# Second attention of a two-layer gated block: the last batch's head layout made on TensorE instead of by DRAM, and its last batches routed in groups of 2, 1 and 1

## The chip, the cores and the metric

The kernel runs on one core of one Trainium2 chip. The metric is the device time of one execution in microseconds (us). The program was run three times; the profile is of one further execution. The engines are TensorE (PE, matmuls into the PSUM memory; its weight loads are shown as PEld), VectorE (DVE), ScalarE (ACT), GpSimd (POOL) and SyncE (SP, which here only issues transfers).

## What is computed

The input x has 16 batches of 128 tokens and 256 features. Two gated layers are applied:

- layer 0: cross-attention with quantized weights and a feed-forward block, each added with a tanh gate;
- layer 1: a second attention and a mixture of eight experts.

The second attention is what matters here. It has 32 heads of 8 features in 8 groups; four heads of a group share keys and values. In the reference, shortened:

```python
q = (Q @ w_q.T).reshape(B, S, G, HG, HD)
k = (K @ w_k.T).reshape(B, S, G, HD)
v = (V @ w_v.T).reshape(B, S, G, HD)
scores = jnp.einsum('bnghd,bmgd->bnghm', q, k) / scale
attn = jax.nn.softmax(jnp.where(causal, scores, NEG_INF), axis=-1)
out = jnp.einsum('bnghm,bmgd->bnghd', attn, v).reshape(B, S, D)
x = x + tanh(g) * (out @ w_o.T + b_o)
```

Then each of the 2048 tokens goes to one expert, by the largest logit. An expert takes at most 256 tokens, in the order of the tokens; so the place of a token in its expert is a running count over all earlier ones. Each expert multiplies its tokens by w1 (256 to 1024), takes gelu, multiplies by w2, and the result is scaled by the gate and added.

## The kernel before, in words

The program goes through the cross-attention (to about 940 us of the span), the feed-forward block (to about 1083), the second attention (to about 1374) and the experts (to the end). The change touches the second attention and its routing.

**Items.** The second attention is a software pipeline over items n = 0 to 63 (the loop at L1192, which runs n from -2 to 70). Item n is batch b = n // 4, half c = n // 2 % 2 of the groups, and pair p = n % 2. An item is two groups of four heads on 128 tokens. In step n of the loop stand `scores(n)` (L1051: mask and scores into PSUM), `top(n)` (L1071: the maximum of each row, on DVE), `probs(n - 1)` (L1087: eight transposes on PE, two copies to eT), `exp(n)` (L1078: eight activations on ACT), `values(n - 2)`, `divide(n - 5)`, and for every fourth step `keys`, `output` and one more stage of each `route` under way.

**Values.** For each odd item, `values` (L1102) multiplies the probabilities of a half, that is four groups q, in one PSUM tile `ps_pv` with one buffer. The weights of a group, `vg` (L1046), are 32 columns wide: value features in the even columns, ones in the odd ones, zero behind. So rows 32q to 32q+15 of the tile hold values and sums in turn, with the four heads side by side along the free axis (512 columns). The output projection needs another layout: one row for each head and feature. So the tile is copied by ACT (`og`, L1115), written by four transfers of SP to DRAM (`ods`, L1119), and read back by one (`ov`, L1127) as 128 rows of 128 values and 128 sums.

**Division and output.** `divide` (L1130) takes the reciprocal of the sums on DVE (L1138) and multiplies on POOL (L1139) into `oT`. `output(b)` (L1141) multiplies both halves of oT with the output weights on PE (L1145), adds the bias (`t`, L1147) and the gated residual (L1151) into the batch's row of a token tile `row`. That tile is made by the first batch of a routing group, from a tag with two buffers. Batch b's output stands in step 4b + 9.

**Routing.** `ROUTES` (L851) lists groups of batches as (first, count). `route` (L855) is a generator of stages, started when the last batch of its group has its output; the loop advances each by one stage a step, and what is left is drained behind the loop (L1223). Its stages: layer norm of the rows (L142 to L148, with two small activations L185 and L186); transposes (L159, L160); logits (L868); softmax, choice of the expert and running count `cum` (L879 to L894); positions by two small matmuls (L897, L898); slots (L903 to L913), then for each batch an indirect scatter of the rows to `disp` in DRAM by POOL (L915) and a plain copy of the row to the output by SP (L926). The running count orders the groups. Before the scatter a copy of token numbers is put into the tile (L910), which also must wait until the tile's buffer is free. In the second attention's PSUM pool the tag "mm" has one buffer, used in the order of the program by query projections, `output`, the logits and the positions.

**Experts.** Each expert's load `xe` (L1244) waits for all scatters, since every token may be among them. The weights of the first two experts are loaded long before.

**Order.** [...] The framework that builds the program orders the instructions by its own estimate of when they are ready, so an engine's queue is not simply the order of the text; the trace shows, for example, the slots of one routing group in turn with the layer norm of the next.

Of the kernel before, what the change touches and what calls it, by code (L numbers as in the profile page):

```python
# [9 lines left out]
F32 = mybir.dt.float32  # L10
# [5 lines left out]
ALU = mybir.AluOpType  # L16
AX = mybir.AxisListType

P = 128
B = 16  # L20
# [15 lines left out]
def flamingo_kernel(  # L36
# [27 lines left out]
    nc = tc.nc  # L64
# [4 lines left out]
    NH, NG, HD = 32, 8, 8  # L69
# [22 lines left out]
    def ps_acc(shape):  # L92
        return ps("acc", shape, 1)
# [160 lines left out]
    with (  # L254
# [80 lines left out]
        class Unit:  # L335
# [164 lines left out]
            def scores(self, c):  # L500
                qT = self.qT.pop(c)
                pscore = ps_sc([P, 4, P])
                for j in range(4):
                    nc.tensor.matmul(  # L504
                        pscore[:, j, :], qT[:, j, :], self.kT[:, 2 * c + j // 2, :],
                        start=True, stop=True,
                    )
                self.sc[c] = pscore

            def top(self, c):  # L510
                mx = small.tile([P, 4], F32, tag="mx", name="mx")
                nc.vector.tensor_reduce(mx, self.sc[c], AX.X, ALU.max, negate=True)  # L512
                self.mx = mx
# [16 lines left out]
            def divide(self, c):  # L530
                e, sums = self.e[c]
                nc.gpsimd.tensor_tensor(  # L532
                    e, e, sums[:, :, None].to_broadcast([P, 4, P]), ALU.mult
                )

            def probs(self, c):
                e, _ = self.e.pop(c)
                pt = ps_tr([P, 4, P])
                for j in range(4):
                    nc.tensor.transpose(pt[:, j, :], e[:, j, :], ident)  # L540
                eT = ap.tile([P, 4, P], F32, tag="eT", name="eT")
                nc.scalar.copy(eT, pt)  # L542
                self.eT[c] = eT

            def values(self, c):
                eT = self.eT.pop(c)
                pv = ps_pv([P, 4, P])
                for g in range(2):
                    gg = 2 * c + g
                    nc.tensor.matmul(  # L550
                        pv[:, 2 * g : 2 * g + 2, :], self.vt[:, gg * P : (gg + 1) * P],
                        eT[:, 2 * g : 2 * g + 2, :], start=True, stop=True,
                    )
                self.pv[c] = pv
# [28 lines left out]
            def output(self, c):  # L583
                if c == 0:
                    self.acc = ps_acc([P, 2 * DM])
                    self.xb = ap.tile([P, DM], F32, tag="xb", name="xb")
                    src = x1[self.b] if self.cross else x_in[self.b]
                    nc.sync.dma_start(out=self.xb, in_=src)
                for j in range(4):
                    h = 4 * c + j  # L590
                    nc.tensor.matmul(  # L591
                        self.acc, self.cat[c // 2][:, h % 8, :], wpr[self.cross, c][:, j, :, :],
                        start=(h == 0), stop=(h == 15),
                    )
# [196 lines left out]
    def down(b, hd, po):  # L791
# [18 lines left out]
    rp = ctx.enter_context(  # L810
        tc.tile_pool(name="r1", bufs=2, side="right", reuse_waits="tile")
    )
    SCALE1 = 1.0 / math.sqrt(HD)
    NQ = NH // NG


    RW = 2 * DM + 2
# [30 lines left out]
    nc.vector.memset(cum, 0.0)  # L848
    slot_s = cp.tile([P, B], I32, name="slot_s")

    ROUTES = ((0, 4), (4, 4), (8, 4), (12, 3), (15, 1))  # L851
    toks = {}
    scatters, plain = [], []

# [74 lines left out]
    cq = f1.enter_context(tc.tile_pool(name="a1c", bufs=1, side="right", reuse_waits="tile"))  # L929
# [32 lines left out]
    vgs = [cq.tile([P, NG, 32], F32, name=f"vg{i}") for i in range(2)]  # L962
    for t in vgs:
        nc.gpsimd.memset(t, 0.0)
        nc.gpsimd.memset(t[:, :, 1 : 2 * HD : 2], 1.0)

    front = {}

    def load(g):
# [63 lines left out]
    kbs, vps, es, eTs, oTs, scs, mxs, ovs = {}, {}, {}, {}, {}, {}, {}, {}  # L1033

    def keys(b):

        g, j = divmod(b, G)
        f = front[g]
        tok = slice(j * P, (j + 1) * P)
        kb = ap.tile([P, KD, NQ, P], F32, tag="kb", name="kb")  # L1040
        for c in range(KD):
            nc.gpsimd.tensor_tensor(
                kb[:, c], f["k"][:, c, None, tok].to_broadcast([P, NQ, P]),
                hmask[:, :, None].to_broadcast([P, NQ, P]), ALU.mult,
            )
        nc.gpsimd.tensor_copy(  # L1046
            vgs[b % 2][:, :, 0 : 2 * HD : 2], f["v"][:, j, :].rearrange("p (g d) -> p g d", d=HD)
        )
        kbs[b], vps[b] = kb, vgs[b % 2]

    def scores(n):  # L1051
# [50 lines left out]
    def values(n):  # L1102

        if n % 2 == 0:
            return
        b, c = n // 4, n // 2 % 2
        o = psum.tile([P, NQ * P], F32, tag="pv", name="ps_pv", bufs=1)
        for q in range(4):
            nc.tensor.matmul(
                o[32 * q : 32 * q + 32, :], vps[b][:, 4 * c + q, :],  # L1110
                eTs[n - 1 + q // 2][:, q % 2].rearrange("p h t -> p (h t)"),
                start=True, stop=True,
            )
        og = ap.tile([P, NQ, P], F32, tag="og", name="og")
        nc.scalar.copy(og.rearrange("p h t -> p (h t)"), o)  # L1115

        od = ods[n // 2]
        for q in range(4):
            nc.sync.dma_start(  # L1119
                out=bass.AP(  # L1120
                    od.tensor, od.offset + 32 * q * 2 * P,
                    [[P, 2 * HD], [2 * HD * P, NQ], [1, P]],
                ),
                in_=og[32 * q : 32 * q + 2 * HD],
            )
        ov = ap.tile([P, 2, P], F32, tag="ov", name="ov")
        nc.sync.dma_start(out=ov.rearrange("p i t -> p (i t)"), in_=od)  # L1127
        ovs[n] = ov

    def divide(n):  # L1130
        if n % 2 == 0:
            return
        b, c = n // 4, n // 2 % 2
        if c == 0:
            oTs[b] = ap.tile([P, KD, P], F32, tag="oT", name="oT")
        ov = ovs.pop(n)
        r = ap.tile([P, P], F32, tag="rsum", name="rsum")
        nc.vector.reciprocal(r, ov[:, 1, :])  # L1138
        nc.gpsimd.tensor_tensor(oTs[b][:, c, :], ov[:, 0, :], r, ALU.mult)  # L1139

    def output(b):  # L1141
        oT = oTs.pop(b)
        pw = psum.tile([P, DM], F32, tag="mm", name="ps_mm")
        for k in range(KD):
            nc.tensor.matmul(pw, oT[:, k, :], ao[:, k, :], start=(k == 0), stop=(k == KD - 1))  # L1145
        t = ap.tile([P, DM], F32, tag="t", name="t")
        nc.vector.tensor_tensor(t, pw, bo, ALU.add)  # L1147
        b0, count = next(r for r in ROUTES if r[0] <= b < r[0] + r[1])
        if b == b0:
            toks[b] = rp.tile([P, count, RW], F32, tag="row", name="row")  # L1150
        nc.vector.scalar_tensor_tensor(  # L1151
            toks[b0][:, b - b0, DM : 2 * DM], t, tg[:, 1:2], x[b], ALU.mult, ALU.add
        )
# [15 lines left out]
    for g in range(B // G):  # L1169
# [3 lines left out]
        for b in range(g * G, (g + 1) * G):  # L1173
# [8 lines left out]
    ap = f2.enter_context(tc.tile_pool(name="a1", bufs=2, side="right", reuse_waits="tile"))  # L1182
    psum = f2.enter_context(
        tc.tile_pool(
            name="psum1", bufs=1, space=bass.MemoryType.PSUM, reuse_waits="tile"
# [3 lines left out]

    N1 = 4 * B  # L1190
    routes = []
    for n in range(-2, N1 + 7):  # L1192
        if 0 <= n < N1:
            scores(n)
            top(n)
        if 0 <= n - 1 < N1:
            probs(n - 1)
        if 0 <= n < N1:
            exp(n)
        if 0 <= n < G:  # L1200
            down(B - G + n, hd, psum.tile([P, DM], F32, tag="mm", name="ps_mm"))
            if n == G - 1:
                tp.close()
                ep = ctx.enter_context(tc.tile_pool(name="e1", bufs=2, reuse_waits="tile"))
        if 0 <= n - 2 < N1:
            values(n - 2)
        if 0 <= n - 5 < N1:
            divide(n - 5)
        m = n + 2
        if m % 4 == 0 and 0 <= m < N1:  # L1210
            keys(m // 4)
        g, i = divmod(n + 12, 16)
        if 1 <= g < B // G:
            front_step(g, i)
        for stages in routes:
            next(stages, None)
        m = n - 6
        if m % 4 == 3 and 0 <= m < N1:
            output(m // 4)
            for b0, count in ROUTES:  # L1220
                if m // 4 == b0 + count - 1:
                    routes.append(route(b0, count))
    for stages in routes:  # L1223
        for _ in stages:
# [6 lines left out]
            name="psum2", bufs=2, space=bass.MemoryType.PSUM, reuse_waits="tile"  # L1231
# [6 lines left out]
    for e in range(NE):  # L1238
# [12 lines left out]
        for f in range(NFC):  # L1251
            ph = ps_mm([P, CAP])
            for k in range(KD):
                nc.tensor.matmul(
                    ph, w1t[:, k, f * P : (f + 1) * P], xT[:, k, :],
                    start=(k == 0), stop=(k == KD - 1),
# [3 lines left out]
        for c in range(NCC):  # L1260
            po = ps_sc([P, DM])
            for f in range(NFC):
                nc.tensor.matmul(
                    po, hT[:, f, c * P : (c + 1) * P], w2t[:, f, :],
                    start=(f == 0), stop=(f == NFC - 1),
# [8 lines left out]
                    ap=xe[:, c, 2 * DM + 1 : 2 * DM + 2].bitcast(I32), axis=0  # L1274
# [79 lines left out]
```

## Time and profile before

| what | value |
|---|---|
| median of 3 runs (lowest to highest) | 1501.8 us (1501.51 to 1504.62) |
| the profiled execution | 1503.01 us |
| its span, first to last instruction | 1501.3 us |
| mean granted TensorE clock | 0.966 |
| PE busy / weight loads | 1369.6 us (91%) / 964.4 us |
| DVE / ACT / POOL busy | 988.6 / 838.4 / 687.6 us |
| og to ods, 128 writes, and ods to ov, 32 reads | 32 KB and 128 KB each |

A profile line gives a start and a duration in us from the span's start, the engine, the line of the code, the operation, written tile <- read tiles, shapes, and how many instructions are merged (x8). In brackets at its end stands how long the engine had been idle before it, and what ended that. PEld is the load of weights for the matmuls of the same line, and SPq or POOLq is an engine's own queue of transfers and waits. One fp32 matmul stands as two records, a transpose as one. "128*32 128x512" is a matmul of 128 rows by 32 columns of weights that streams 512 columns.

### The profile page before, as it was taken

The page shows a single profiled execution, that of the slowest core. Times are in us where ns is not written, and L with a number is a line of the kernel's source. Part 1 is how long each engine was busy: PE and PEld are TensorE (multiplying, and loading weights), DVE is VectorE, ACT ScalarE, POOL GpSimd, SP SyncE. Part 2 cuts the span into 40 slices and gives each one's busy share as a digit, 9 for nine tenths or more (in the row PEclk, how much of TensorE's full clock was granted, in tenths as well). Part 3 has the DMA queues.
Part 4 walks back from the last instruction along what each step waited for, and adds up shares of the span by engine and source line. Part 5 has one row for each costly group of instructions (what it writes and reads, how often), then busy time and mean ns, then how long its engine had stood idle before and what let it go on. Part 6 is the DMA issues. An engine that isn't in the chain of part 4 may idle for free. (4 is left out here: it accounts for less than half of the span.)

```text
span 1501.3 us, 21652 instructions
## 1 busy us (share of the span) xinstructions
PE 1369.6 (91%) x6852; PEld 964.4 (64%) x6852; DVE 988.6 (66%) x2597; ACT 838.4 (56%) x2496; POOL 687.6 (46%) x615
## 2 busy tenths in 40 slices
PE   2789899899988999999999997999999999985998
PEld 1578778687776777777777766555544444444887
DVE  7867878778689777777676764453478787762100
ACT  3666566666656676666666663164476575741221
POOL 4476677677766565656556563121032322111111
PEclk9699999999999999999999998899999999986999
DMA  4300101000013100000000000700042212122652
GB/s 133 110 17 23 38 22 38 21 22 27 22 55 104 45 29 19 15 16 17 12 18 15 15 4 27 211 8 14 31 128 53 75 50 63 40 75 76 196 189 70
DMA packets 78770, 80.37 MB, mean 54 GB/s; under 512 B 15291, under 2 KB 64891, under 8 KB 78656
## 3 DMA queue, kind: packets, MB, share of 16 engines
q1 hardware_dynamic: 65152, 55.29, 12.7%
q10 hardware_dynamic: 11456, 17.63, 3.6%
q0 software_dynamic: 2048, 6.07, 1.1%
q8 instruction: 55, 0.90, 0.3%
q14 instruction: 59, 0.48, 0.1%
HBM read 57.14 MB, written 22.05 MB: 53 GB/s over the span
## 5 line engine op out<-in xcount | busy, mean ns | idle before, releaser
L532 POOL TENSOR_TENSOR e<-e,sums 128x512 f32<-128x512 f32 x128 | 141.4, 1105 | 239.7 <-DVE sums L528 100.8
L475 POOL TENSOR_TENSOR raw<-raw,q_r 128x512 f32<-128x512 f32 x192 | 211.3, 1126 | 21.0 <-DVE q_r L312 19.6
L520 ACT ACTIVATE e<-ps_sc,mx 128x128 f32<-128x128 f32 x512 | 181.1, 368 | 63.6 <-DVE mx L512 58.1
L452 DVE BATCH_NORM_STATS2 q_st<-raw 128x6 f32<-128x128 f32 x768 | 174.2, 279 | 64.2 <-ACT raw L443 63.6
L591 PE MATMUL ps_acc<-wp,cat 128*128 128x512 f32 x512 | 159.3, 433 | 14.0 <-POOL cat L237 13.4
L504 PE MATMUL ps_sc<-kT,qT 128*128 128x128 f32 x1024 | 140.9, 281 | 23.9 <-ACT qT L495 23.9
L542 ACT COPY eT<-ps_tr 128x512 f32<-128x512 f32 x128 | 75.3, 588 | 156.3 <-PE ps_tr L540 156.3
L504 PEld LDWEIGHTS ps_sc<-kT,qT 128*128 128x128 f32 x1024 | 132.4, 194 | 44.1 <-ACT qT L495 36.6
L237 POOL TENSOR_TENSOR cat<-e_t,e_e 128x1024 fp32r<-128x1024 bf16 x64 | 136.6, 2135 | 43.5 <-DVE e_t L231 43.5
L1082 ACT ACTIVATE e<-ps_sc,mx 128x128 f32<-128x128 f32 x512 | 139.0, 392 | 30.5 <-DVE mx L1073 30.1
L550 PE MATMUL ps_pv<-eT,vt 128*128 128x256 f32 x512 | 133.8, 383 | 1.0 <-DVE cat_y L561 1.0
L443 ACT COPY raw<-ps_mm 128x512 f32<-128x512 f32 x192 | 113.8, 593 | 29.2 <-PE ps_mm L431 25.8
L591 PEld LDWEIGHTS ps_acc<-wp,cat 128*128 128x128 f32 x512 | 94.6, 191 | 53.4 <-POOL cat L237 20.1
L486 PE MATMUL ps_tr<-ident,raw 128*128 128x128 f32 x768 | 115.2, 276 | 13.6 <-POOL raw L475 11.6
L486 PEld LDWEIGHTS ps_tr<-ident,raw 128*128 128x128 f32 x768 | 91.6, 141 | 47.5 <-POOL raw L475 20.5
L561 DVE TENSOR_TENSOR cat_y<-ps_pv,r_sm 128x512 bf16<-128x512 f32 x128 | 87.1, 680 | 47.2 <-PE ps_pv L550 46.7
L550 PEld LDWEIGHTS ps_pv<-eT,vt 128*128 128x128 f32 x512 | 97.3, 192 | 30.9 <-issue 10.5
L512 DVE TENSOR_REDUCE mx<-ps_sc 128x4 f32<-128x512 f32 x128 | 87.2, 682 | 38.5 <-PE ps_sc L504 37.8
L495 ACT ACTIVATE qT<-ps_tr,hv 128x512 f32<-128x512 f32 x128 | 101.2, 791 | 19.9 <-PE ps_tr L486 17.7
L520 ACT ACTIVATION_READ_ACCUMULATOR e<-ps_sc,mx 128x1 f32 x512 | 105.4, 206 | 0.0
L1093 PEld LDWEIGHTS ps_tr<-ident,e 128*128 128x128 f32 x512 | 59.9, 142 | 64.9 <-ACT e L1082 28.1
L1073 DVE TENSOR_REDUCE mx<-ps_sc 128x8 f32<-128x1024 f32 x64 | 77.6, 1212 | 30.2 <-PE ps_sc L1066 20.9
(221 smaller groups left out, 2687.0 us busy)
## 6 DMA issues: line engine op xcount, KB each, us to landing
w1t<-in_w ACTq DMA_DIRECT2D x8, 1024.0 KB
w2t<-in_w ACTq DMA_DIRECT2D x8, 1024.0 KB
disp<-empty SPq DMA_DIRECT2D x16, 257.0 KB
xe<-disp SPq DMA_DIRECT2D x8, 514.0 KB
ctx<-in_ctxT SPq DMA_DIRECT2D x32, 128.0 KB
stage<-in_wprojT SPq DMA_DIRECT2D x16, 256.0 KB
ods<-og SPq DMA_DIRECT2D x128, 32.0 KB
ov<-ods SPq DMA_DIRECT2D x32, 128.0 KB
```

What stands on the lines that cost most here:

```text
L237: ins = nc.gpsimd.tensor_tensor(dst, t[:, part], e[:, part], ALU.subtract)
L443: nc.scalar.copy(raw.rearrange("p h d -> p (h d)"), pm)
L452: nc.vector.bn_stats(self.st[:, 4 * blk + j, :], self.raws[blk][:, j, :])
L475: ins = nc.gpsimd.tensor_tensor(src, src, self.r[:, 4 * blk : 4 * blk + 4, None].to_broadcast([P, 4, P]), ALU.mult,)
L486: nc.tensor.transpose(pt[:, j, :], src[:, j, :], ident)
L495: nc.scalar.activation(dst, pt, AF.Identity, scale=hv[:, col : col + 1], bias=hv[:, col + 1 : col + 2])
L504: nc.tensor.matmul(pscore[:, j, :], qT[:, j, :], self.kT[:, 2 * c + j // 2, :], start=True, stop=True,)
L520: nc.scalar.activation(e[:, j, :], pscore[:, j, :], AF.Exp, bias=self.mx[:, j : j + 1], accum_out=sums[:, j : j + 1],)
L532: nc.gpsimd.tensor_tensor(e, e, sums[:, :, None].to_broadcast([P, 4, P]), ALU.mult)
L550: nc.tensor.matmul(pv[:, 2 * g : 2 * g + 2, :], self.vt[:, gg * P : (gg + 1) * P], eT[:, 2 * g : 2 * g + 2, :], start=True, stop=True,)
L591: nc.tensor.matmul(self.acc, self.cat[c // 2][:, h % 8, :], wpr[self.cross, c][:, j, :, :], start=(h == 0), stop=(h == 15),)
L1082: nc.scalar.activation(e[:, i, :], s[:, i // NQ, i % NQ, :], AF.Exp, bias=mx[:, i : i + 1])
```

## The change

Three things are changed.

- For the last batch, `values` makes the final layout at once. The values of a group stand in four copies of 32 columns, copy h with the features in columns 8h to 8h + 7 and zeros elsewhere (`vpad`); `ones8` is the same with ones. For each half, the four heads are accumulated in PSUM: 16 matmuls of 128 columns give the values, 16 more the sums. `divide` is called at once and reads both from PSUM, with both of its steps on DVE; the copy, the five transfers and the POOL product of a half are not there for this batch.
- Routing groups (12, 3) and (15, 1) become (12, 2), (14, 1) and (15, 1); groups of one batch use a tag `row1` with two buffers of its own.
- The loop ends at n = 65. Outputs of batches 14 and 15 both stand in its last step, before what is left of the routings is drained. Batch 14's output was already in step 65, batch 15's was in step 69.

```diff
-    ROUTES = ((0, 4), (4, 4), (8, 4), (12, 3), (15, 1))
+    ROUTES = ((0, 4), (4, 4), (8, 4), (12, 2), (14, 1), (15, 1))
...
+    ones8 = cq.tile([P, NQ, 32], F32, name="ones8")
+    vpad = cq.tile([P, NG, NQ, 32], F32, name="vpad")
+    nc.gpsimd.memset(ones8, 0.0)
+    for i in range(NQ):
+        nc.gpsimd.memset(ones8[:, i, HD * i : HD * i + HD], 1.0)
+    nc.gpsimd.memset(vpad, 0.0)
...
-        nc.gpsimd.tensor_copy(
-            vgs[b % 2][:, :, 0 : 2 * HD : 2], f["v"][:, j, :].rearrange("p (g d) -> p g d", d=HD)
-        )
+        v = f["v"][:, j, :].rearrange("p (g d) -> p g d", d=HD)
+        if b < B - 1:
+            nc.gpsimd.tensor_copy(vgs[b % 2][:, :, 0 : 2 * HD : 2], v)
+        else:
+            vp = vpad[:]
+            nc.gpsimd.tensor_copy(
+                bass.AP(vp.tensor, vp.offset, [vp.ap[0], [P, NG], [32 + HD, NQ], [1, HD]]),
+                v[:, :, None, :].to_broadcast([P, NG, NQ, HD]),
+            )
...
         o = psum.tile([P, NQ * P], F32, tag="pv", name="ps_pv", bufs=1)
+        if b == B - 1:
+            for t in range(2):
+                for h in range(NQ):
+                    for q in range(4):
+                        lhs = (vpad[:, 4 * c + q, h, :], ones8[:, h, :])[t]
+                        nc.tensor.matmul(
+                            o[32 * q : 32 * q + 32, t * P : (t + 1) * P], lhs,
+                            eTs[n - 1 + q // 2][:, q % 2, h, :],
+                            start=(h == 0), stop=(h == NQ - 1),
+                        )
+            divide(n, o)
+            return
...
-    def divide(n):
-        if n % 2 == 0:
+    def divide(n, o=None):
+        if n % 2 == 0 or (n // 4 == B - 1 and o is None):
             return
...
+        r = ap.tile([P, P], F32, tag="rsum", name="rsum")
+        if o is not None:
+            nc.vector.reciprocal(r, o[:, P : 2 * P])
+            nc.vector.tensor_tensor(oTs[b][:, c, :], o[:, :P], r, ALU.mult)
+            return
         ov = ovs.pop(n)
...
-            toks[b] = rp.tile([P, count, RW], F32, tag="row", name="row")
+            tag = "row" if count > 1 else "row1"
+            toks[b] = rp.tile([P, count, RW], F32, tag=tag, name=tag)
...
-    for n in range(-2, N1 + 7):
+    for n in range(-2, N1 + 2):
...
-        if m % 4 == 3 and 0 <= m < N1:
-            output(m // 4)
+        if n == N1 + 1:
+            ready = [B - 2, B - 1]
+        else:
+            ready = [m // 4] if m % 4 == 3 and 0 <= m // 4 < B - 2 else []
+        for b in ready:
+            output(b)
             for b0, count in ROUTES:
-                if m // 4 == b0 + count - 1:
+                if b == b0 + count - 1:
                     routes.append(route(b0, count))
```

More of the change, by code (lines that the diff above doesn't have):

```diff
@@ L1135, in divide @@
             oTs[b] = ap.tile([P, KD, P], F32, tag="oT", name="oT")
+        r = ap.tile([P, P], F32, tag="rsum", name="rsum")
[3 more added lines that the diff above has]
+            return
         ov = ovs.pop(n)
-        r = ap.tile([P, P], F32, tag="rsum", name="rsum")
         nc.vector.reciprocal(r, ov[:, 1, :])
```

## The prediction

> **What bounds the kernel now.** I read the page first: its chain that ended last covers only the final 15 us (issue, an output scatter), so it says nothing of the middle. Part 2 shows TensorE (PE) at 9 of 10 nearly everywhere, with a dent (5, then 9) near slice 36, where the granted clock falls too. Busy time by engine in 10 us stretches puts the dent where the change works:
>
> ```profile
> 1320.00:1330.00 10.00, 10.00 (x54) 4.16 (x54) 8.24 (x18) 7.94 (x27) 4.39 (x5) 1.00 0.32 105
> 1330.00:1340.00 10.00, 8.28 (x41) 3.88 (x38) 5.54 (x9) 5.40 (x18) 0.45 (x1) 0.83 0.22 67
> 1340.00:1350.00 10.00, 5.91 (x29) 3.59 (x26) 5.51 (x15) 2.06 (x5) 0.45 (x1) 0.80 0.25 67
> 1350.00:1360.00 10.00, 4.83 (x15) 3.17 (x14) 5.85 (x27) 0.22 (x1) 0.91 (x2) 0.50 0.04 15
> 1360.00:1370.00 10.00, 2.71 (x10) 2.15 (x10) 4.44 (x29) 0.88 (x4) 3.88 (x4) 0.50 0.27 105
> 1370.00:1380.00 10.00, 5.44 (x16) 4.18 (x17) 0.08 (x1) 2.79 (x5) 0.00 (x0) 0.50 0.32 105
> ```
>
> The columns are the stretch, its length, PE, weight loads, VectorE (DVE), ScalarE (ACT) and GpSimd (POOL) busy, the clock, the DMA share and GB/s. Until 1330 PE is full; from 1332 to 1374 nothing is. This is the drain of the second attention: latency bounds it, and the experts behind it can't start. A microsecond of this chain is a microsecond of the span. The timeline of the drain, cut to the links:
>
> ```profile
> 1331.81 0.15 DVE L910 COPY row<-number 128x1 int32<-128x1 int32 x1 [1.83 <-DMA disp<-row,slot_s]
> ...
> 1334.30 4.23 ACT L1082 ACTIVATE e<-ps_sc,mx 128x128 f32<-128x128 f32 x16 [2.17 <-DVE mx L1073]
> 1334.72 1.99 PEld L1093 LDWEIGHTS ps_tr<-ident,e 128*128 128x128 f32 x8 [2.55 <-ACT e L1082]
> ...
> 1336.93 0.20 PEld L1109 LDWEIGHTS ps_pv<-eT,vg 128*32 128x32 f32 x8 [0.22 <-issue]
> 1336.93 1.94 PE L1109 MATMUL ps_pv<-eT,vg 128*32 128x512 f32 x8
> ...
> 1340.50 1.79 PE L1109 MATMUL ps_pv<-eT,vg 128*32 128x512 f32 x8
> ...
> 1342.33 0.58 ACT L1115 COPY og<-ps_pv 128x512 f32<-128x512 f32 x1 [1.14 <-DMA ods<-og]
> ...
> 1347.05 0.34 SPq L1127 DMA_DIRECT2D ov<-ods  x1
> ...
> 1348.60 2.73 PE L868 MATMUL ps_mm<-wgt,rT 128*128 128x8 f32 x12 [0.35 <-ACT rT L160]
> 1351.37 0.18 DVE L879 TENSOR_REDUCE gmx<-ps_mm 128x3 f32<-128x24 f32 x1 [2.53 <-PE ps_mm L868]
> ...
> 1354.82 0.95 DVE L1138 RECIPROCAL rsum<-ov 128x128 f32<-128x128 f32 x1
> 1355.85 0.45 POOL L1139 TENSOR_TENSOR oT<-ov,rsum 128x128 f32<-128x128 f32 x1 [1.57 <-DVE rsum L1138]
> ...
> 1357.61 0.42 DVE L1147 TENSOR_TENSOR t<-ps_mm,bo 128x256 f32<-128x256 f32 x1 [1.85 <-PE ps_mm L1145]
> ```
>
> ```profile
> 1367.78 0.96 POOL L915 DMA_INDIRECT disp<-row,slot_s  x1 [3.34 <-DVE slot_s L913]
> 1370.78 28.55 SPq L1244 DMA_DIRECT2D xe<-disp  x3
> 1374.53 0.71 PEld L159 LDWEIGHTS ps_tr<-ident,xe 128*128 128x128 f32 x4 [8.36 <-DMA xe<-disp]
> ```
>
> Read downwards: the last values end at 1340.50 + 1.79 = 1342.29; their way by DRAM is issued back at 1347.05; the reciprocal starts only at 1354.82; oT of batch 15 is ready at 1356.30; its row has t at 1358.03, is scattered at 1367.78, and the experts begin at 1374.53. So the DRAM way is less than half of the 14.0 us from values to oT: the read of batch 15's first half, issued at 1344.72, releases POOL's wait at 1346.82, 2.1 us later, so the second landed near 1349.2. The rest is DVE's order: the reciprocal stands behind the softmax of group 12 to 14, which itself waits 2.53 us for PE at half clock.
>
> **The change, part by part.** The sum is made in the profiled execution, 1503.01 us with a span of 1501.3 and 1.7 around it; the median of the three runs is 1501.8, and I carry the difference over to it.
>
> *A. A buffer wait goes, and routing of 12 and 13 comes forward.* The first row above is the token tile of batch 15 taking the buffer of batches 8 to 11 and waiting for their scatters. All of DVE's queue stood behind it: max of item 62, then exp (ACT idle 2.17) and PE (2.55). The new tag has its own buffers: up to -1.8. But group (12, 2) now starts after batch 13 (t at 1329.04) and its norm falls into the same stretch: aggregation 0.17, sum 0.17, four small ones of 0.16, two rows of 0.41, 1.8 us of DVE, and two ACT ones of 0.20. Its transposes, logits (8 records of 0.112 at full clock, from L868's sixteen in 1.85) and some 13 small DVE operations of 0.18 fall into DVE gaps (2.44 us idle before 1340.17). If the norm is ahead of an item's max, all of the gain goes, and a us more; if the gaps take it, none. I take -1.0, ends -2.2 and +1.0.
>
> *B. More and smaller matmuls.* Four matmuls of 128x512 (eight records, two each) become 32 of 128x128, 64 records, twice: the zero-padded columns give each head its rows and double what is streamed. Per column group two records of 512 columns become sixteen of 128: 1024 columns to 2048. The same L1109 form takes 1.07 us for eight at full clock (1294.16) and 1.94 at half. With 0.17 for filling, double is 1.97 or 3.7: +0.9 or +1.8 for each half. The first half stands on PE between the transposes of items 62 and 63, the second starts when both copies of item 63's probabilities are there (1341.19) and no longer partly before. I take +1.3 and +0.9, together +2.2. The low end is +0.9: without A's gap PE may keep its clock, and 1.97 costs nothing against 1.94.
>
> Here a rule speaks against the change. The Trainium skill, "TensorE: Matmul & The Clock Gate", Part 3, The mechanism, says that a weight load overlaps a running matmul only when its row group differs; ours all use 128 rows. By that rule each record waits for its load: 16 x (0.107 + 0.27, the trace's load and 128-column matmul) = 6.1 us a half at full clock, 12.2 - 3.7 = +8.5 for both instead of +2.2. The row says otherwise: eight loads are over in 0.20 us while matmuls with 1.06 each run. I take the row; the same page's Part 2 allows a background buffer. The rule's value is the high end.
>
> *C. The way by DRAM goes.* Away: the og copy, four writes and a read on SP's queue for each half, and the POOL product. New on DVE: a reciprocal from PSUM, 0.95 as now from SBUF, and a product of 128x128 from PSUM: L1147's 128x256 is 0.42 and tiny ones 0.16, so 0.29. With handoffs 1.3 us from values to oT. The new wait: psum1's "mm" tag has one buffer, and output(14) stands right ahead of output(15) in it; its second oT half came at 1342.25, no earlier than the last values. I put it behind them: 0.9 us of PE, then t of batch 14 behind both division steps on DVE, 0.42. Output(15) starts 1.8 us after the values instead of 14.0: -12.2. If output(14) slips ahead: -12.7. If the division again stands 5.6 us behind a softmax (1354.82 - 1349.2): -6.6. The first half's division also frees the one "pv" buffer for the second half: 1.3 us after 1338.87 is 1340.2, before 1341.19, so hidden by the copies; if B's first half runs at half clock it shows with about 1 us. The vpad copy replaces POOL's 0.29 us copy with about 0.55 (between it and the 512-element product, 1.06), in idle of 5.5 us before it; it no longer waits for PE. The six new memsets, about 1.5 us (514 columns took 0.53), lie near 940 on a POOL used 1 to 3 tenths there: nothing; uncovered 1.5.
>
> *D. Two routings at the end instead of one.* Scatter of 15 follows t15 by 9.75 us now. Then positions of 12, logits and positions of 14, and logits of 15 go one after another through the single "mm" buffer: 1.3 (pl12, 1358.03 to 1359.36) + 3.6 (lg to position read, 1362.90 to 1366.47) + 4.9 (1362.90 to 1367.78) = 9.8. Norm and transposes of 15 (4.9 after t15) lie beside the first two. But DVE has some 7 us of small operations in those 4.9; about 1.9 of it delays 15: +1.9. Low end 0 (all interleave, as 12 to 14 and 15 do now); high end +7, when 14 goes through before 15's norm begins. SP's extra row copy and POOL's scatters (1.27 apart) keep their number and have slack: nothing, one scatter more in line 1.3.
>
> Sum: -1.0 + 2.2 - 12.2 + 1.9 = -9.1; 1503.0 becomes 1493.9, and the median 1501.8 becomes **1492.7**. From the scatter on, all shifts: landing, xe load, a cold first expert, which has its weights.
>
> **The rivals.** *The routings and divisions queue up* (D at +7, or C at -6.6): -4.0, 1497.8. For: DVE is in order, and softmax stood ahead of the reciprocal. Against: the orders of the two routings interleave now. *Weight loads are not hidden* (the rule): -2.8, 1499.0, no change that shows. *Slower: the small matmuls do not run side by side in the column groups.* Then 64 records follow each other at L868's spacing, 0.214 at half clock: 13.7 us a half, 27.4 - 3.7 = +23.7 for B against -11.3 for the rest: +12.4, 1514. It decides from (3.7 + 11.3)/128 = 0.117 us a record, just above L868's 0.112 at full clock. Against: L1109's eight run together today. *It does not do what it says*, DRAM way hidden anyway: excluded but for the landing part, since the reciprocal starts late for DVE's order as well; that is the first rival.
>
> **How the numbers follow.** Forecast case 0.62 (1489 to 1495.5: A and D at their ends); queueing 0.20; loads not hidden, or another loss that cancels, 0.11; serial matmuls or a new wait elsewhere from shifted buffers and reordered queues, 0.07. About 0.2%, 3.0 us, is what a measurement can tell from none, so 1498.8 is the border of faster: 0.87; within 0.07; slower 0.06 (some of the unhidden loads at half clock). The range takes forecast and queueing, 1488.8 to 1498.8.
>
> **What would show it.** A: no DVE wait on disp near 1330, exp of 62 and 63 some 1.8 us earlier, less what group 12's norm takes. B: each batch-15 group of 64 records lasts 2 us (full) or 3.7, not 6 or more. C: output(15) within 2 us of the last values, and output(14)'s t between. D: the last scatter 11 to 12 us after t15. The drain's end, 1374.5 now, near 1365. Wrong if DVE or PE at 1330 to 1350 waits for the division, if PE before 1330 is no longer full, or if the records don't overlap.

## The result, and the profile after

The changed kernel takes 1494.03 us (median of five runs, 1491.8 to 1494.53) against 1501.8 before (median, now of five runs too); the ratio is 0.9933, 95% interval 0.9919 to 0.9948. Forecast were 1492.7 us and "faster". The interval stands for 7.8 to 12.2 us saved, so it is faster; 9.1 us were forecast. The two medians alone differ by 7.8 us, which is the low edge of that interval. The profiled execution took 1494.03 us with a span of 1492.3, so 9.0 us less span than before.

Busy time by engine in stretches of 10 us, with the columns as before:

```profile
1330.00:1340.00 10.00, 9.25 (x104) 5.62 (x103) 9.37 (x20) 5.85 (x22) 0.91 (x2) 1.00 0.28 85
1340.00:1350.00 10.00, 6.78 (x90) 5.16 (x89) 8.64 (x47) 1.88 (x7) 1.48 (x3) 0.85 0.08 26
1350.00:1360.00 10.00, 4.14 (x17) 3.54 (x17) 4.75 (x39) 0.58 (x3) 2.88 (x3) 0.50 0.20 79
1360.00:1370.00 10.00, 4.11 (x11) 3.18 (x12) 0.00 (x0) 2.41 (x4) 0.00 (x0) 0.50 0.40 134
```

The clock holds at 1.00 through 1330 to 1340, where it was 0.83, and DVE is busy 9.37 of 10 us there (5.54 before): the drain's first part is now filled with work of DVE and of PE (9.25) where a stall was. The drain is one stretch shorter, with the experts starting inside the last of these.

The links of the drain from the timeline:

```profile
1330.01 0.42 DVE L1178 TENSOR_TENSOR t<-ps_mm,bo 128x256 f32<-128x256 f32 x1 [1.37 <-PE ps_mm L1176]
...
1335.67 2.16 ACT L1097 ACTIVATE e<-ps_sc,mx 128x128 f32<-128x128 f32 x8
1335.74 0.81 PEld L1128 LDWEIGHTS ps_pv<-eT,vpad 128*32 128x32 f32 x32
1335.74 1.08 PE L1128 MATMUL ps_pv<-eT,vpad 128*32 128x128 f32 x32
...
1338.09 0.67 PE L159 MATMUL ps_tr<-ident,row 128*128 128x128 f32 x4 [0.39 <-DVE row L148]
...
1339.12 1.09 PE L1108 MATMUL ps_tr<-ident,e 128*128 128x128 f32 x8 [0.35 <-ACT rT L160]
...
1341.83 1.06 PE L1128 MATMUL ps_pv<-eT,ones 128*32 128x128 f32 x32
...
1343.05 0.96 DVE L1165 RECIPROCAL rsum<-ps_pv 128x128 f32<-128x128 f32 x1
1343.98 0.42 DVE L1178 TENSOR_TENSOR t<-ps_mm,bo 128x256 f32<-128x256 f32 x1
1344.33 0.28 DVE L1166 TENSOR_TENSOR oT<-ps_pv,rsum 128x128 f32<-128x128 f32 x1
...
1345.63 0.42 DVE L1178 TENSOR_TENSOR t<-ps_mm,bo 128x256 f32<-128x256 f32 x1 [0.17 <-PE ps_mm L1176]
...
1349.60 1.03 PE L868 MATMUL ps_mm<-wgt,rT 128*128 128x8 f32 x4
1353.75 1.00 PE L868 MATMUL ps_mm<-wgt,rT 128*128 128x8 f32 x4 [0.35 <-DVE prev L893]
...
1356.15 0.57 PE L897 MATMUL ps_mm<-oh,before 128*128 128x8 f32 x2 [1.40 <-DVE slot L907]
...
1358.66 0.96 POOL L915 DMA_INDIRECT disp<-row,slot_s  x1 [1.76 <-DVE slot_s L913]
1362.11 0.89 SPq L1280 DMA_DIRECT2D xe<-disp  x2
1365.85 0.72 PEld L159 LDWEIGHTS ps_tr<-ident,xe 128*128 128x128 f32 x4 [8.80 <-DMA xe<-disp]
```

Read downwards: t of batch 13 at 1330.01; the last values end at 1341.83 + 1.06 = 1342.89; t of batch 15 ends at 1346.05, 3.2 us later where it was 15.75; the last scatter starts at 1358.66; the experts begin at 1365.85 (forecast: near 1365). No wait on `disp` is left near 1330.

One caution decides how runs are compared. Over the profiled executions of this study batch 13's t starts anywhere from 1325.0 to 1331.0, and in the changed kernel it starts 0.97 us later than before; 0.60 of that is there at 92 us already, long before anything of the edit runs. So I compare *drains*: from the start of batch 13's t to the first transposes of the experts. What follows it lasts 125.8 to 127.1 us in every run. The change's 9.0 us are then +0.97 before the drain, -9.65 in it (45.49 to 35.84) and -0.3 after it. The six new memsets and the `vpad` copy, which the prediction put at nothing, show no cost in it: batch 13's t starts at 1328.2 us on average in the nine profiles that have them, and at 1328.7 in the three without.

A second caution holds for the ends of drains. The clock falls to 0.50 at 17.0 us after the start of batch 13's t in the changed kernel's first profile and at 17.3 in e5, but at 19.8 in the changed kernel's second profile and in e9. Ends are therefore best compared with the profile whose clock falls at the same place.

All runs, in us. "V" is the end of the last values, counted like t15 (end of batch 15's t) from the start of batch 13's t:

| run | V | V to t15 | t15 to last scatter | drain | ratio to before (95%) |
|---|---|---|---|---|---|
| before | 13.25 | 15.75 | 9.74 | 45.49 | 1 |
| changed | 12.87 | 3.17 | 12.60 | 35.84 | 0.9933 (0.9919 to 0.9948) |
| changed, run again | 12.87 | 3.17 | 12.25 | 35.42 | 0.9932 (0.9919 to 0.9944) |
| e1 groups and tag only | 12.53 | 11.77 | 9.66 | 40.70 | 0.9962 (0.9948 to 0.9977) |
| e2 tag only | 10.02 | 15.75 | 9.74 | 42.40 | 0.9974 (0.9967 to 0.9982) |
| e3 direct values only | 14.90 | 2.94 | 16.60 | 41.58 | 0.9980 (0.9971 to 0.9989) |
| e4 records group by group | 20.40 | 3.17 | 12.41 | 43.09 | 0.9988 (0.9979 to 0.9996) |
| e5 own bank for 15's routing | 12.88 | 3.17 | 11.62 | 34.87 | 0.9921 (0.9908 to 0.9933) |
| e6 14 and 15 as a pair, tag "row" | 15.27 | 3.17 | 12.02 | 37.92 | 0.9947 (0.9936 to 0.9959) |
| e7 turn of 12 one stage later | 12.55 | 4.79 | 12.13 | 36.62 | 0.9935 (0.9921 to 0.9949) |
| e8 old groups, new tag | 11.61 | 2.94 | 16.61 | 38.58 | 0.9956 (0.9939 to 0.9973) |
| e9 pair, tag of its own | 12.87 | 3.17 | 11.92 | 35.13 | 0.9928 (0.9907 to 0.9949) |

### The profile page after: what moved, and what is told of

Same layout as the page of the kernel before. It is cut to its first block, busy times and chain, and to the rows that moved or that the text cites. A ratio compares the mean times of both kernels' runs of the same rounds, so it can differ in the third digit from the quotient of the medians.

```text
span 1492.3 us, 21897 instructions
## 1 busy us (share of the span) xinstructions
PE 1365.4 (91%) x6968; PEld 963.5 (65%) x6968; DVE 991.2 (66%) x2622; ACT 839.3 (56%) x2499; POOL 688.4 (46%) x619
## 3 DMA queue, kind: packets, MB, share of 16 engines
q1 hardware_dynamic: 64224, 54.76, 12.8%
```

## The experiments

The theory was that of the prediction: a stall of DVE at the head of the drain and 14 us between values and output(15) go, and more records and a longer end give some back. The rivals: the records are not hidden beside each other; the gain is the regrouping's alone; the end is bound by the single "mm" buffer.

**The changed kernel again**, beside e5 to e7.

> The changed kernel once more, beside the others on one chip. If its steps are set by the program and not by the run: 35.8 us from batch 13's t to the first expert, within 0.3, while the way there differs by a microsecond or two from run to run; about 1493.5 us.

Measured: median 1490.5 us, 3 less than expected, and drain 35.42 us, just outside the 0.3. V and t15 lie within 0.01 us of the first profile, so up to t15 drains can be compared this finely. The end moved by 0.35 us: the logits of batch 14 took 0.69 us instead of 1.03, since the clock fell only while they ran.

```profile
1344.46 0.69 PE L868 MATMUL ps_mm<-wgt,rT 128*128 128x8 f32 x4 [0.24 <-ACT rT L160]
```

**e1: the new groups and the new tag, the DRAM way kept.** The edit is before, with

```diff
-    ROUTES = ((0, 4), (4, 4), (8, 4), (12, 3), (15, 1))
+    ROUTES = ((0, 4), (4, 4), (8, 4), (12, 2), (14, 1), (15, 1))
...
-            toks[b] = rp.tile([P, count, RW], F32, tag="row", name="row")
+            tag = "row" if count > 1 else "row1"
+            toks[b] = rp.tile([P, count, RW], F32, tag=tag, name=tag)
```

> The kernel before with only the routing groups (12, 2), (14, 1), (15, 1) and the tag of its own for single batches; the values of the last batch still go by DRAM and batch 15's output still stands in step 69. Theory (the DRAM way is less than half of the 14 us from values to oT, the rest is DVE's order behind the softmax of group 12 to 14): with that softmax earlier, the reciprocal starts when the read lands, near 1349, so batch 15's t comes 5 us earlier, the buffer wait of 1.8 us goes, and batch 14 is routed beside the DRAM way: -5 to -7 us in all, and 6 to 8 us from the last values to oT. Rival (the DRAM way carries the gain): only the buffer wait goes, -1 to -2 us.

Measured: drain 40.70, 4.8 us less than before. Without any direct values, V to t15 fell from 15.75 to 11.77. Its timeline shows what is left:

```profile
1338.63 1.06 PE L1109 MATMUL ps_pv<-eT,vg 128*32 128x512 f32 x6
...
1344.84 0.34 SPq L1127 DMA_DIRECT2D ov<-ods  x1
...
1347.85 0.20 DVE L909 TENSOR_SCALAR row<-s,tg 128x1 f32<-128x1 f32 x1
...
1348.24 0.95 DVE L1138 RECIPROCAL rsum<-ov 128x128 f32<-128x128 f32 x1
...
1351.04 0.42 DVE L1147 TENSOR_TENSOR t<-ps_mm,bo 128x256 f32<-128x256 f32 x1 [1.84 <-PE ps_mm L1145]
```

The values end at 1339.70 and the read of the last half is issued at 1344.84, 5.1 us later; with the 2.1 us of landing taken in the prediction it was there near 1347 (an estimate). The reciprocal still stands behind batch 14's softmax until 1348.24. The smaller group costs DVE about 1.3 us there where the group of three cost 5.6: of the 14.0 us, about 4 were DVE's order. The prediction read that cause rightly but gave it more: 6 to 8 us from the last values to oT were expected, and it took 10.0 (oT is ready at 1349.72).

**e2: the tag alone** (the second part of e1's edit, with the old `ROUTES`).

> The kernel before with only the tag of its own for the token tile of batch 15; groups stay (12, 3) and (15, 1). Theory: DVE's wait of 1.8 us near 1330 goes and nothing fills its place, so exp of item 62 starts 1.8 us earlier and the drain is 1.8 us shorter: -1 to -2 us. Rival (the time is given back behind it, since the reciprocal waits for the softmax of group 12 to 14 anyway): 0 to -0.5.

Measured: V at 10.02 instead of 13.25, drain 3.1 us shorter, for a wait of 1.83 us; 1 to 2 were expected. DVE took its queue in order: the next reciprocal, which stands behind the waiting copy, starts 2.87 us after batch 13's t in the kernel before and 0.86 us after it here. A stretch, the last exp and the two groups of values show where the rest comes from:

```profile
1330.00:1340.00 10.00, 9.98 (x55) 4.55 (x53) 7.74 (x12) 5.98 (x20) 1.22 (x3) 1.00 0.32 87
```

```profile
1335.61 1.07 PE L1109 MATMUL ps_pv<-eT,vg 128*32 128x512 f32 x8
...
1335.73 1.66 ACT L1082 ACTIVATE e<-ps_sc,mx 128x128 f32<-128x128 f32 x6
...
1338.11 1.79 PE L1109 MATMUL ps_pv<-eT,vg 128*32 128x512 f32 x8
```

PE no longer stands idle for exp, keeps clock 1.00, and the first half's values take 1.07 us instead of 1.94. Of the 3.23 us at V, 2.0 are there when the last exp ends (9.50 to 7.51); the other 1.2 come between exp and V, where PE works at full clock. e3 against e8 repeats this test with the new values, as the two differ in the tag alone: V falls by 3.29 us and the drain by 3.0.

**e3: direct values alone.** The changed kernel with both parts of e1's edit turned back.

> The changed kernel with the old routing groups (12, 3) and (15, 1) and the old tag; the last batch's values and sums still come from PSUM and the loop still ends at 65. Theory (the parts overlap): values end 1 to 2 us later than before, oT follows within 2 us, but logits, positions of 12 to 14 and logits of 15 then go one after another through the one PSUM buffer: last scatter some 14.5 us after batch 15's t, -5 to -6.5 us in all. Rival (the DRAM way carries nearly the whole gain, the routing groups add only the buffer wait): -7 to -8.

Measured: drain 41.58, 3.9 us less than before, where 5 to 6.5 were expected. Direct values took 12.8 us out between V and t15, but 6.9 came back behind t15 (16.60 us to the last scatter, 14.5 expected). The first half's records ran at the lower clock, 2.96 us in all:

```profile
1336.88 1.94 PE L1128 MATMUL ps_pv<-eT,vpad 128*32 128x128 f32 x32
...
1338.59 1.25 PE L1128 MATMUL ps_pv<-eT,ones 128*32 128x128 f32 x32
...
1346.30 0.42 DVE L1178 TENSOR_TENSOR t<-ps_mm,bo 128x256 f32<-128x256 f32 x1 [0.17 <-PE ps_mm L1176]
...
1351.11 2.73 PE L868 MATMUL ps_mm<-wgt,rT 128*128 128x8 f32 x12 [0.35 <-ACT rT L160]
...
1363.32 0.96 POOL L915 DMA_INDIRECT disp<-row,slot_s  x1 [0.30 <-issue]
```

Before, the routing of 12 to 14 ran while batch 15 was on its way through DRAM. Now both arrive together: the logits of three batches at half clock and then three scatters, 1.27 us apart, stand ahead of the last scatter, which waits for nothing but POOL's queue.

**e4: the same records, one column group after the other.** The changed kernel with

```diff
-            for t in range(2):
-                for h in range(NQ):
-                    for q in range(4):
+            for q in range(4):
+                for t in range(2):
+                    for h in range(NQ):
```

> The changed kernel with the matmuls of the last batch's halves in another order: all 16 of one column group, then the next group, in place of the four groups in turn. Same matmuls, same count. Theory (four column groups run side by side only while their matmuls alternate): a half lasts 4 x 16 x 0.107 = 6.9 us in place of 1.96, both on the path, some +8 to +10 us against the changed kernel, so about 1502 to 1504, no faster than before. Rival (the matmuls overlap whatever their order, or the load hides it): a half stays near 2 us and the time near 1494.

Measured: 5.95 us a half instead of 1.95 (6.9 expected), drain 7.3 us longer than the changed kernel's, ratio 0.9988 (0.9979 to 0.9996) to before: only a trace of the gain is left.

```profile
1332.87 1.06 PE L1128 MATMUL ps_pv<-eT,vpad 128*32 128x128 f32 x8
...
1337.79 1.04 PE L1128 MATMUL ps_pv<-eT,ones 128*32 128x128 f32 x8
...
1338.93 0.96 DVE L1165 RECIPROCAL rsum<-ps_pv 128x128 f32<-128x128 f32 x1 [3.54 <-PE ps_pv L1128]
```

In one group eight records take about 1.05 us, one every 0.11; in the changed kernel 32 records take 1.08, four groups abreast. So the rival of serial small matmuls is a real danger, and the order of the loops decides it; here it stays short of slower, since its records run at full clock and not at the 0.214 us of half clock on which the rival counted. It cost less than 64 x 0.11 = 7.0 us because neighbouring groups overlap at their borders.

**e5: batch 15's logits and positions in a bank of their own** (the scores' tag, free by then).

```diff
-        lg = ps("mm", [P, G, NE], 1)
+        lg = ps(*(("sc", [P, G, NE], 2) if b0 == B - 1 else ("mm", [P, G, NE], 1)))
...
-        pl = ps("mm", [P, G, NE], 1)
+        pl = ps(*(("sc", [P, G, NE], 2) if b0 == B - 1 else ("mm", [P, G, NE], 1)))
```

> The changed kernel with logits and positions of batch 15's routing in another PSUM tag (that of the scores, which is free by then), so that they no longer wait for those of batch 14. Theory (the single PSUM buffer makes the 12.6 us from batch 15's t to the last scatter): its logits start about 1351.6 in place of 1353.75, and the last scatter comes 1.5 to 2.2 us earlier. Rival (DVE's small operations of three routings make it): the logits start earlier, but their softmax waits on DVE; at most 0.7 us.

Measured: t15 to last scatter 11.62 us, 0.6 to 1.0 less than the changed kernel, between what theory and rival expected; drain 34.87. Against the first profile, whose clock falls at the same place, it is 1.0.

```profile
1348.35 1.03 PE L868 MATMUL ps_mm<-wgt,rT 128*128 128x8 f32 x4
...
1350.04 1.02 PE L868 MATMUL ps_sc<-wgt,rT 128*128 128x8 f32 x4
...
1353.88 0.60 PE L897 MATMUL ps_sc<-oh,before 128*128 128x8 f32 x2 [1.21 <-DVE slot L907]
```

The logits of 15 follow those of 14 by 1.69 us instead of 4.15, so the buffer did hold them 2.5 us. But their positions then come 3.84 us behind the logits instead of 2.40: the small operations of both routings share DVE. The buffer was worth about 1.0 of the 2.9 us that the end grew by; the rest I put down to DVE, which no run shows by itself.

**e6: 14 and 15 routed together**, `(12, 2), (14, 2)`. A group of two takes the tag "row", so the wait on the buffer came back with it (2.01 us).

> The changed kernel with batches 14 and 15 as one routing group, (12, 2) and (14, 2). Theory (the cost of two routings at the end is about what one of twice the size costs: the logits double at half clock, and the second scatter stands 1.27 us behind the first): 12.2 us from t to the last scatter in place of 12.6, no difference that a time can show. Rival (running two chains one behind the other costs all of the 2.9 us over the 9.7 of before): -1.5 us or more.

Measured: drain 37.92. The wait hides the answer: V at 15.27, 2.4 us later than in the changed kernel. t15 to last scatter is 12.02, no gain that shows. As a test of pairing it is confounded; it confirms e2 from the other side.

```profile
1335.80 2.29 PE L1108 MATMUL ps_tr<-ident,e 128*128 128x128 f32 x8 [1.90 <-ACT e L1097]
```

PE waits 1.90 us for exp again, and the eight transposes behind it take 2.29 us where they took 1.91.

**e7: the turn of group (12, 2) one stage later**, to let the last item's transposes go first.

```diff
         layer_norm(rp, [row[:, j, DM : 2 * DM] for j in range(G)], y)
-        yield
+        yield from [None] * (1 + (b0 == 12))
```

> The changed kernel with the stages of group (12, 2) behind its norm one step later, so that its transposes stand behind the last item's on PE and its softmax beside the division. Theory (bringing the routing forward costs 1 to 1.3 us, since its transposes and copies hold the two buffers that the last item's transposes wait for): the last values end 1 us earlier, and most of it is lost or kept depending on where the softmax falls: -1 us in the drain. Rival (the last values wait for exp or for the division of the half before): no change at the last values.

Measured: V only 0.33 us earlier, t15 1.3 us later, drain 36.62, which is nearer to the rival than to the theory.

```profile
1340.57 0.27 DVE L1166 TENSOR_TENSOR oT<-ps_pv,rsum 128x128 f32<-128x128 f32 x1
...
1341.59 1.08 PE L1128 MATMUL ps_pv<-eT,vpad 128*32 128x128 f32 x32
```

The transposes did go first, but the first half's division came later, and the last values wait for it, since "pv" has one buffer. Softmax of 12 and 13 then stands before output(14)'s t: what was moved off one link landed on the next.

**e8: the old groups with the new tag**, direct values kept (the changed kernel with the old line of `ROUTES`).

> The changed kernel with the routing groups of before (12 to 14 together, 15 alone) while batch 15's token tile keeps the tag with buffers of its own and its values keep the direct way. It differs from the changed kernel in the groups alone. Theory (routing of 12 and 13 brought forward costs some 2.5 us at the last values, and buys it back at the end, because one scatter of three tiles and a routing of three batches no longer stands ahead of batch 15's): last values end 10.2 to 10.8 us after t of batch 13 starts, against 12.87 in the changed kernel; the last scatter follows t of batch 15 by about 16.6 us as in the run with direct values alone, against 12.4; drain 37 to 38 us against 35.6, so 1.5 to 2 us slower than the changed kernel and about 6 faster than before. Rival (the 2.5 us come from the tag's other effects, not from the routing that comes forward): last values end near 12.5, drain 39 to 40, 4 us slower than the changed kernel.

Measured: V at 11.61, between the two theories' numbers, drain 38.58. The forward routing costs 12.87 - 11.61 = 1.3 us here, not 2.5.

```profile
1334.59 1.09 PE L1108 MATMUL ps_tr<-ident,e 128*128 128x128 f32 x8
...
1336.21 0.27 DVE L1166 TENSOR_TENSOR oT<-ps_pv,rsum 128x128 f32<-128x128 f32 x1
...
1336.63 1.08 PE L1128 MATMUL ps_pv<-eT,vpad 128*32 128x128 f32 x32 [0.52 <-DVE oT L1166]
```

The transposes of the last item start 7.62 us after batch 13's t and not 9.11, so they gain 1.5 us. Then the division of the first half becomes the last wait, because that one buffer is given back only at 1336.48. From t15 to the experts the old groups lose 4.2 us; their last scatter comes 16.61 us after t15, as in e3.

**e9: the pair with a token tile of its own** (as e6, with the tag "row1" and one buffer for the group of 14 and 15).

> The changed kernel with batches 14 and 15 routed as one group of two, whose token tile has a buffer of its own, so that it doesn't wait for the scatter of 8 to 11. It repeats the pairing run without the buffer wait that came back in it. Theory (the two routings at the end cost what DVE's small operations cost, and pairs do not need fewer of those on the path): last values end at 12.9 us after t of batch 13 as in the changed kernel, last scatter 12.0 us after t of batch 15, drain 35.3 to 35.9: no difference from the changed kernel that shows. Rival (two separate routings through one PSUM buffer cost 1.9 us or more, and one routing saves it): last scatter 10 to 10.5 us after t of batch 15, drain near 33.5, 2 us faster than the changed kernel.

Measured: V at 12.87 as in the changed kernel, t15 to last scatter 11.92, drain 35.13. No difference from the changed kernel that shows, as the theory had it.

```profile
1347.33 1.87 PE L868 MATMUL ps_mm<-wgt,rT 128*128 128x8 f32 x8 [0.25 <-ACT rT L160]
...
1354.42 0.96 POOL L915 DMA_INDIRECT disp<-row,slot_s  x1 [0.30 <-issue]
```

The pair saves one round of small operations, but its logits take 1.87 us at half clock instead of 1.00, and its second scatter stands 1.27 us behind its first.

e5 and e9 have the shortest drains, 0.3 to 1.0 us below the changed kernel's. Their ratios overlap its interval, so neither is shown to be faster than it; both are faster than before.

## Why the prediction was right, point by point

The sum was -9.1 us; the drain gave -9.65 and, run again, -10.07. The sum held better than its terms, and that is luck in part: by the first profile the terms were off by -1.6 at V, -0.4 in C, +1.0 in D and +0.45 at the end, and most of that cancels. The forecast time differs from the measured median by 1.3 us. Nearly all of it is the base: the profile before, in which the sum was made, lay 1.2 us above the median of its runs, and the profile after lies at its median.

| step | forecast | measured |
|---|---|---|
| A and B, at V | -1.0 + 2.2 = +1.2 | -0.38 (13.25 to 12.87) |
| C, V to t15 | -12.2 | -12.58 (15.75 to 3.17) |
| D, t15 to last scatter | +1.9 | +2.86 and +2.51 |
| last scatter to experts | 0 | +0.45 |

*A, mis-sized in both of its terms.* "Up to -1.8" was the length of the wait. e2 shows -3.2 at V, as the wait also cost PE its clock (the tag alone takes the stretch from 0.83 to 1.00). The routing that comes forward was to cost 0.8 of that. It costs 2.5 with the old values (e1 against e2) and 1.3 with the new ones (the changed kernel against e8). The prediction looked for it in DVE's queue, and it does load DVE there; but what holds the last item is PE: its transposes start behind the four of the tokens and the release of their buffers by ACT, `[0.35 <-ACT rT L160]` at 1339.12. A alone thus comes to -0.7 or -2.0, by which values it is measured with; the -1.0 lies between by luck of two errors.

*B, right in the mechanism, and smaller.* The 64 records take 1.95 us at full clock, as worked out (1.97). Since A keeps the clock, the first half costs nothing against 1.94: the low end. On the path the new values cost +1.6 without the forward routing (e2 to e8) and +0.3 with it (e1 to changed), against +2.2. The 1.6 is mainly a later start: the old half began 8.2 us after batch 13's t and the new one at 9.7, since its first four records need both copies of the last item, and the division must have freed the buffer. With the forward routing the start is late anyway. The weight loads lie beside the matmuls (0.81 in 1.08), so the rule weighed in the prediction is not borne out for four column groups in turn; its sum would have been 6.0 us a half (16 x 0.377; the prediction has 6.1) and V near 13.25 - 1.0 + 8.5 = 20.7. e4 looks like that: 5.95 and 20.40. But there the records of one group follow each other at 0.11 us and not at the 0.38 of load and matmul in turn, so it shows serial matmuls, not waiting loads. The prediction took a like figure, 0.112, from L868, whose records stream 8 columns where these stream 128; that both have one cause is not shown.

*C, right.* The reciprocal starts 0.16 us after V, and t of batch 14 stands between it and the product, as written. Shown by e1 and the changed kernel: the DRAM way was worth 11.77 - 3.17 = 8.6 us, and DVE's order behind the old group 15.75 - 11.77 = 4.0. The division was called hidden by the copies; so it is in the changed kernel (product over at 1340.09, last copy at 1340.83, values at 1340.93), but with the old groups (e3, e8) and the late turn (e7) it is the last wait.

*D, under-sized by 0.6 to 1.0.* The delay was put at 1.9 us of DVE's work, and the sign named for it, 11 to 12 us from t15 to the last scatter, was missed (12.60 and 12.25). e5 shows that the single buffer makes about 1.0 of the growth, and e9 that pairing does not avoid the rest. And the base was the wrong one: 9.74 could not stay once batch 15 arrives early. With the old groups the end takes 16.6 us (e3, e8). So the regrouping that the prediction booked as a cost of 1.9 saves 4.2 from t15 to the experts, and loses 1.5 ahead of t15 (14.55 to 16.04): 2.7 us net, 38.58 against 35.84.

*The parts together.* e1 saves 4.8 us and e3 3.9, which makes 8.7; both saved 9.65. That is not plain addition. Between V and t15 they overlap: 4.0 + 12.8 = 16.8 in the sum, 12.6 together, as DVE's order counts in both. Behind t15 they help each other: e3 alone loses 6.9 there, together they lose 2.9. At V they do too: -0.7 and +1.65 apart, -0.4 together, since e3's 64 records still ran at the lower clock (2.96 us for its first half).

*Left open.* The 0.45 us from the last scatter to the experts: all runs with direct values have 3.35 to 3.7 us from scatter to the load of xe, where before had 3.00; I have not told its cause apart. Nor is it settled why the forward routing costs 1.2 us more with the old values, beyond that its logits stand right ahead of them on PE in e1. And the 6 us over which batch 13's t wanders from profile to profile (1325.0 to 1331.0) were not studied.

## What to carry to other kernels

In a drain, price a wait by what starts late and by the clock that is lost behind it, and not by its length alone: here 1.83 us were worth 3.1. When a step on the path is removed, look at what used to run in its shadow, as the work hidden there (here a routing of three batches) comes out at the end, and shrink that in the same change. Here many small matmuls kept the pace of few large ones (64 records of 128 columns in 1.95 us, 8 of 512, half of the columns, in 1.07) only in an order that lets the column groups run abreast: put the loop over groups innermost, and look in the trace at the time of a whole group of records.

## What was not expected of the hardware

- A stall of DVE of 1.8 us, through 2.2 us of idle ACT and 2.5 of idle weight loads, took the granted clock of that 10 us stretch from 1.00 to 0.83. The eight records behind it took 1.94 us instead of 1.07 (before against e2). The PE wait ahead of it was 1.73 us, by the gap between its records. In all three kernels that keep the wait (before, e3, e6) the clock is 0.50 from 1336 to 1338; in the nine others it stays at 1.00 for at least 13.7 us after the start of batch 13's t.
- 64 records of 128 columns to four column groups in turn took 1.95 us; the same records group after group took 5.95 (changed against e4).
- A reciprocal of 128x128 took 0.96 us from PSUM as from SBUF (0.95), and the product from PSUM 0.23 to 0.29 (estimated 0.29).
